# A graph layer on one core: the gathers' extra wait is taken out, and four list slots of two tiles of the seventh pair become one-hot products

## The chip, the cores and the metric

One Trainium2 chip, of which the kernel uses one core. The metric is device time in microseconds; a kernel's time is the median of its runs. The engines are TensorE (PE, with its weight loads PEld), VectorE (DVE), ScalarE (ACT), GpSimd (POOL) and SyncE (SP, which here only issues transfers).

## What is computed

16 graphs of 1024 nodes with 64 channels and a 0/1 adjacency (about 9 neighbours a node). Each node's own row is layer-normed and cut at zero; some edges are dropped by a rule on their rank; over a node's remaining neighbours (itself among them) three quantiles of each channel are taken and weighted; a small MLP follows.

```python
h = jnp.maximum(_layernorm(x, axis=-1), 0.0)
neigh = (adj_ > 0) & ~eye
rank = jnp.cumsum(ni, axis=-1) - ni
...
rem = neigh & (sk > 1) & (rank % sk == sk - 1) & mask[:, :, None]
rem = rem | jnp.swapaxes(rem, 1, 2)
adj_d = jnp.where(rem, 0.0, adj_)
...
s = jnp.sort(vals, axis=2)
for tau, w in zip((0.25, 0.5, 0.75), (0.25, 0.5, 0.25)):
    pos = tau * (nv - 1)
    ...
    agg = agg + w * (v_lo + frac * (v_hi - v_lo))
out = h + agg
y = jax.nn.relu(out @ W1 + b1) @ W2 + b2
return x + y * mask
```

## The kernel before

**Stages.** The graphs (batches 0 to 15) go in pairs (0 to 7). For each batch, `load` takes the adjacency in eight tiles of 128 rows, `drop` and `keep` find the edges that stay, `order` sorts the nodes by their number of neighbours, and `collect` writes for each node the list of its neighbours' numbers: `lists[b]`, the tile idx, which is done at L1186. The normed rows h go to a table in HBM, gtab.

**Gathers.** A pair's sorted nodes stand in eight tiles of 128 nodes, in four classes (`CLASSES`, L65): tile 0; tiles 1, 2, 3; tiles 4, 5; tiles 6, 7. For each class there is a buffer in SBUF, g0, g1, g4 and g6, with a slot for each place in the list; g0 and g1 exist twice, g4 and g6 once. One gather (L1329, an indirect transfer that POOL prepares) fills one slot of one tile of one graph: 128 rows of 64 values, by one column of the list. A pair needs 126 of them; the last pair 70.

**Picks.** For the last pair (pair 7) the first slots of tiles 0 to 5 (`LEAST`, L67: 8, 4, 4, 4, 4, 4) are not gathered. Every node there has that many neighbours, and the rows are taken from SBUF instead: `begin_pick` (L1344) loads the two graphs' table from HBM (xt), splits each value into three bf16 terms (terms) and turns the list into f32 (index). `pick` (L1370) works in rounds of eight slots. PE spreads eight list columns over the partitions (rowsT), ACT copies them (rows), DVE compares them with the node numbers in eight instructions of 128x1024 (hot, L1389), PE multiplies hot by the terms (got, L1398, 64 products a round), and ACT puts the bytes of got into the slots (L1409, L1410). There are seven rounds. hot has one buffer, shared with other tiles of the tag "wide"; index has the two buffers of the tag "keys".

**Sorts.** `sort` (L1414) runs a sorting network over a class's slots with DVE's min and max (L1437, L1442, L1434); the wanted places are weighted (L1457 on ACT, L1459 on DVE) and summed by PE (L1463). Behind many of DVE's instructions `opened` (L853) sets a memset of one column, called pause. 32 nodes of each graph with very many neighbours are sorted apart, eight graphs at a time, in gg. `one_hot`, `sums` and `mlp` bring the result back to node order and make the output.

**The order.** `weave` decides only which instruction is written down first. Then `arrange` (L713) takes all instructions as a graph of dependencies, buffers among them, with a cost for each (`Step.cost`), and makes each engine's order by walks forwards and backwards over it (`ROUNDS`, L74); the walk with the shortest total stands. The order of each engine is fixed from then on. Behind the walks, two waits are set on POOL: each gather waits for the count of those issued before it (`paced`), and, the leash (L785 to L794), for a DVE instruction: the latest among those with waiters on other engines that the plan ends more than 25000 ns (`LEASH`) ahead of the gather's planned start.

```python
    shown = [s for s in sequence["DVE"] if s.tells]
    for s in sequence["POOL"]:
        while len(shown) > 1 and starts[shown[1].place] + shown[1].busy < starts[s.place] - LEASH:
            shown.pop(0)
```

The main loop (L1830) weaves the results of pair m - 1 with the lists of pair m + 1; at m = 7 the picks stand in place of the lists.

Of the kernel before, what the change touches and what calls it, by code (L numbers as in the profile page):

```python
# [47 lines left out]
NT = N // P  # L48
# [16 lines left out]
CLASSES = (((0,), 13), ((1, 2, 3), 11), ((4, 5), 9), ((6, 7), 7))  # L65

LEAST = (8, 4, 4, 4, 4, 4, 0, 0)  # L67
# [3 lines left out]
GROUP = 8  # L71
SLICE = P // GROUP
SECOND = 14
ROUNDS, LEASH = 6, 25000  # L74


TURNED = (0, 1, 3, 2, 0, 1, 3, 2)
# [635 lines left out]
def arrange(tc, runs, loose, tails, paced):  # L713

    steps, found, number = [], {}, {}
    for ins in list(tc.nc.cur_bb.bb.instructions):
        if type(ins).__name__.startswith("BassTile"):
            continue
        if ins.name in tails:
            at = found[ins.name] = found[tails[ins.name]]  # L720
            at.tail.append(ins)
            number[ins.name] = len(number)
            at.busy += 12
            continue
        found[ins.name] = Step(ins, len(steps))
        steps.append(found[ins.name])

    written, read, users, order = {}, {}, {}, {}
    for s in steps:
        for u in s.reads + s.writes:  # L730
            name = u.tile.name
            for o, other in written.get(name, ()):
                if u.meets(other):
                    s.before.add(o.place)
            for o, other in read.get(name, ()) if u in s.writes or u.psum else ():
                if u.meets(other):
                    (s.before if u in s.writes or o.engine != s.engine else s.behind).add(o.place)
        for u in s.writes:
            for table in (written, read):
                table[u.tile.name] = [e for e in table.get(u.tile.name, ()) if not u.covers(e[1])]  # L740
            written[u.tile.name].append((s, u))
        for u in s.reads:
            read.setdefault(u.tile.name, []).append((s, u))
        for u in s.reads + s.writes:
            if getattr(u.tile, "tag", None):
                if u.tile.name not in users:
                    order.setdefault(u.tile.tag, []).append(u.tile)
                users.setdefault(u.tile.name, []).append(s)
    for tiles in order.values():
        for k, t in enumerate(tiles):  # L750
            bufs = t.tag_meta.bufs
            first = users[t.name][0]
            if k:
                first.behind.add(users[tiles[k - 1].name][0].place)
            if k >= bufs:
                first.before.update(o.place for o in users[tiles[k - bufs].name])
            for o in users[t.name][1:]:
                if o is not first:
                    o.behind.add(first.place)
    close = {found[n].place: (found[run[0]].place, found[run[-1]].place) for run in runs for n in run[:-1]}  # L760
    for s in steps:
        for first, last in {close[p] for p in s.before if p in close}:
            if not first <= s.place <= last:
                s.before.add(last)
    for s in steps:
        s.behind -= s.before
        s.before.discard(s.place)
        s.behind.discard(s.place)
        for p in (*s.before, *s.behind):
            steps[p].after.append(s)  # L770

    for s in steps:
        s.tells = any(o.engine != s.engine for o in s.after if s.place in o.before)
    ranks, best = [float(s.place) for s in steps], None
    for _ in range(ROUNDS):
        sequence, starts, total = forward(steps, ranks)
        if best is None or total < best[0]:
            best = total, sequence, starts
        ranks = backward(steps, starts)
    _, sequence, starts = best  # L780

    for k, s in enumerate(s for s in sequence["POOL"] if s.ins.name in paced[1]):
        if k > 1:
            paced[1][s.ins.name].wait_op(paced[0], k - 1, "sem-ge")
    shown = [s for s in sequence["DVE"] if s.tells]  # L785
    for s in sequence["POOL"]:
        while len(shown) > 1 and starts[shown[1].place] + shown[1].busy < starts[s.place] - LEASH:
            shown.pop(0)
        if s.ins.name in paced[1] and starts[shown[0].place] + shown[0].busy < starts[s.place] - LEASH:
            tc.add_manual_dep(  # L790
                s.ins, shown[0].ins.name,
                mybir.DependencyInfo(mybir.DependencyClass.Sync, mybir.DependencyReason.DATA),
                reason="leash of the gathers",
            )  # L794
    for steps in sequence.values():
        alike = iter(sorted((i for s in steps for i in s.tail), key=lambda i: number[i.name]))
        line = [i for s in steps for i in (s.ins, *(next(alike) for _ in s.tail))]
        at = {ins.name: k for k, ins in enumerate(line)}
        for ins in line:
            if ins.name in loose and at[loose[ins.name]] < at[ins.name] - 1:  # L800
                tc.declare_no_dep(ins, loose[ins.name], reason="read in order by one engine")
        for ins, then in zip(line, line[1:]):
            tc.add_manual_dep(
                then, ins.name, mybir.DependencyInfo(mybir.DependencyClass.NoSync, mybir.DependencyReason.DATA),
                reason="order of the engine",
            )
# [3 lines left out]
def list_layer(  # L810
# [494 lines left out]
            turn[0] += 1  # L1305
            many = None if many is None else many - 1

    def opening(some, m=B // 2 - 1):

        tiles, slots = some  # L1310
        if (m, tiles) not in gathered:
            gathered[m, tiles] = wk.tile(
                [P, PLANS[slots][0], len(tiles), 2, C], F32, name=f"g{tiles[0]}", bufs=2 - tiles[0] // 4
            )

    def fetch(m, classes=CLASSES, halves=(0, 1)):

        for tiles, slots in classes:
            lo, n = tiles[0], len(tiles)
            held, order = PLANS[slots][:2]  # L1320

            def begin(h, tiles=tiles, lo=lo, n=n, slots=slots, held=held):
                opening((tiles, slots), m)
                nc.scalar.copy(gathered[m, tiles][:, slots - 1, :, h], owns[m][:, lo:lo + n, h])

            issued, given_out = paced

            def gather(h, slot, k, at, tiles=tiles, lo=lo):
                ins = nc.gpsimd.indirect_dma_start(  # L1329
                    out=gathered[m, tiles][:, slot, k - lo, h], out_offset=None, in_=tables[2 * m + h][0],  # L1330
                    in_offset=bass.IndirectOffsetOnAxis(ap=lists[2 * m + h][:, at:at + 1], axis=0),
                    element_offset=tables[2 * m + h][1], engine_sem=issued,
                )
                given_out[ins.ins.name] = ins
                return ins

            for h in halves:
                queue.append(partial(begin, h))
                for k in tiles:
                    for s, slot in enumerate(order[:FULL[k] + ((k, FULL[k]) in HOSTS)]):  # L1340
                        if m < pairs - 1 or s >= LEAST[k]:
                            queue.append(partial(gather, h, slot, k, PASSED[k] + s))

    def begin_pick():  # L1344

        first = wk.tile([P, NT], F32, name="first", bufs=1)
        nc.vector.tensor_tensor(first, own2.rearrange("p (t k) -> p t k", k=2)[:, :, 0], own2.rearrange("p (t k) -> p t k", k=2)[:, :, 1], OP.add)
        nc.vector.tensor_scalar(first, first, float(FRONT), None, OP.add)
        terms, index = [], []
        for h in range(2):  # L1350
            b = 2 * (pairs - 1) + h
            xt = wk.tile([P, NT, C], F32, name="xt", bufs=1)
            tab, at = tables[b]
            nc.sync.dma_start(
# [10 lines left out]
            f = wk.tile([P, PASSED[-1]], F32, name="index", tag="keys", bufs=2)  # L1365
            nc.scalar.copy(f, lists[b])
            index.append(f)
        return first, terms, index

    def pick(first, terms, index, wanted):  # L1370

        m = pairs - 1
        for n in range(0, len(wanted), 8):
            some = wanted[n:n + 8]
            rows = wk.tile([P, len(some), P], F16, name="rows", tag="dist", bufs=2)
# [16 lines left out]
            for at in range(0, len(some), 2):  # L1392
# [8 lines left out]
                    )  # L1401
                    for q in range(2) for j in range(NT)
                ])
                opening((tiles, slots))
                step = to[1] - to[0]
                end = to[1] + (1 if step > 0 else -1)
                line = gathered[m, tiles][:, to[0]:end if end >= 0 else None:step, k - tiles[0], h]
# [379 lines left out]
    def drain(*gens):  # L1787
        for g in gens:
            for _ in g:
                pass  # L1790
# [39 lines left out]
    for m in range(pairs + 1):  # L1830
# [15 lines left out]
            nc.vector.tensor_scalar(flag, fp, 0.0, None, OP.is_gt)  # L1846
        side = chain(*(prepare(b) for b in (2 * m + 2, 2 * m + 3) if b < B))
        if m == pairs - 1:
            side = pick(*begin_pick(), [
                (h, k, s) for tiles, _ in CLASSES[:3] for h in range(2) for k in tiles for s in range(LEAST[k])  # L1850
            ])
            for _ in range(20):
                next(side)
# [190 lines left out]
```

## Time and profile before

| | us |
|---|---|
| median of 3 runs | 1918.85 |
| the runs | 1901.87, 1927.52, 1918.85 |
| the profiled execution: its time | 1901.87 |
| its span, first to last instruction | 1900.1 |
| granted TensorE clock, mean | 0.809 |
| gathers (L1329) | 952, mean 1.039 |
| one-hot compares (L1389) | 56, median 0.480 |
| products of the picks (L1398) | 448 |
| lists of batches 12 to 15 done at (L1186) | 1349.7, 1376.5, 1528.6, 1593.0 |
| sort of pair 6: g0, g1, g4, g6 (first to last step starts) | 1567 to 1648, 1647 to 1696, 1698 to 1723, 1723 to 1736 |
| gathers of pair 6: g0, g1, g4, g6 | 1484 to 1524, 1524 to 1624, 1624 to 1679, 1679 to 1705 |
| gathers of pair 7 and of gg | 1705 to 1852 |
| last sort step starts | 1879.1 |

How to read it: the profile is of one execution, and times in it count from its first instruction. A row of a group gives line, engine, operation, out <- in, count, busy time and mean in ns of one, then the idle time of the engine just before the group and what ended it. A row of the waits gives the total in us, how often, and the longest. "issue" and "remote" name no engine. A row of the timeline ends with the idle time before it and its releaser in brackets. The stretches give each engine's busy time and the number of its instructions.

### The profile page before, as it was taken

How to read it: one execution, taken by the hardware profiler on the slowest of the kernel's cores; microseconds unless marked ns; L12 is line 12 of the kernel's file. 1: busy time of each engine (PE TensorE's matmuls, PEld its weight loads, DVE VectorE, ACT ScalarE, POOL GpSimd, SP SyncE). 2: the span in 40 equal slices, each digit the busy share in tenths (PEclk: the TensorE clock that was granted, in tenths of full speed). 3: DMA queues.
4: the chain of work that ended last, by engine and by line, in shares of the span. 5: the costliest groups of instructions: out<-in, count | busy, mean ns of one | idle time of the engine just before them, and what ended most of it. 6: DMA issues, size and time to landing. Idle time of an engine off the chain costs nothing. (4 is left out here: it accounts for less than half of the span.)

```text
span 1900.1 us, 30251 instructions
## 1 busy us (share of the span) xinstructions
PE 1228.6 (65%) x8995; PEld 770.5 (41%) x9011; DVE 1226.8 (65%) x5869; ACT 1069.1 (56%) x2869; POOL 1027.3 (54%) x991
## 2 busy tenths in 40 slices
PE   6637566577867587667664687655873678733847
PEld 4424344254444344344432444433542345511434
DVE  5515277653676758774658658586757745596895
ACT  7646356466663578355662657353673675323765
POOL 0354564644564646554557455465565645577780
PEclk9769689597888798878877798767986789866868
DMA  5423232212331214121322123231230110112110
GB/s 185 137 76 92 61 92 67 83 50 68 84 102 43 86 39 137 42 73 45 102 79 50 54 47 104 54 94 32 54 71 18 31 21 20 19 23 49 27 31 15
DMA packets 128832, 121.67 MB, mean 64 GB/s; under 512 B 95730, under 2 KB 96274, under 8 KB 128658
## 3 DMA queue, kind: packets, MB, share of 16 engines
q1 hardware_dynamic: 97106, 87.29, 15.3%
q0 software_dynamic: 31552, 32.36, 8.7%
q8 instruction: 73, 1.20, 0.3%
q14 instruction: 101, 0.83, 0.1%
HBM read 108.79 MB, written 9.05 MB: 62 GB/s over the span
## 5 line engine op out<-in xcount | busy, mean ns | idle before, releaser
L1329 POOL DMA_INDIRECT g<-gtab,idx x952 | 989.4, 1039 | 816.3 <-issue 211.8
L1437 DVE TENSOR_TENSOR g<-g 128x384 f32<-128x384 f32 (+2 forms) x659 | 310.9, 492 | 25.1 <-issue 10.7
L1442 DVE TENSOR_TENSOR g<-g 128x384 f32<-128x384 f32 (+2 forms) x659 | 310.1, 491 | 10.1 <-DMA gg<-g 6.0
L1142 PE MATMUL codeP<-pack,perm 128*128 128x332 bf16 x1024 | 191.7, 332 | 59.2 <-DVE perm L1117 38.3
L1045 ACT ACTIVATE dist<-rk,bias 128x512 f16<-128x512 f32 x256 | 169.2, 701 | 84.5 <-remote 44.2
L1068 ACT ACTIVATE kept<-kp 128x512 fp8e4<-128x512 f32 x224 | 133.4, 600 | 132.9 <-remote 61.1
L978 ACT ACTIVATE ne<-tp 128x512 fp8e4<-128x512 f32 x248 | 143.4, 612 | 102.7 <-remote 67.4
L965 PE MATMUL tp<-kb,sg 128*128 128x128 bf16 x1024 | 119.9, 250 | 98.7 <-issue 37.5
L1463 PE MATMUL acc<-g,kf 128*128 128x128 f32 (+2 forms) x472 | 146.2, 446 | 55.7 <-ACT g L1457 35.5
L1035 PE MATMUL rk<-kb,cnt 128*128 128x512 bf16 x256 | 113.7, 444 | 93.6 <-ACT dist L1045 47.4
L1142 PEld LDWEIGHTS <-perm 128*128 128x128 bf16 x1024 | 100.1, 105 | 151.5 <-DVE perm L1117 49.4
L1040 PEld LDWEIGHTS <-ne 128*128 128x128 fp8e4 x1024 | 91.0, 110 | 154.7 <-issue 131.1
L1046 DVE TENSOR_SCALAR rem<-dist,half 128x1024 bf16<-128x1024 f16 x128 | 62.9, 493 | 129.4 <-ACT dist L1045 120.0
L965 PEld LDWEIGHTS <-sg 128*128 128x128 bf16 x1024 | 89.2, 113 | 140.8 <-issue 119.6
L1071 PE MATMUL code<-kw,kept 128*128 128x17 fp8e5 x1024 | 66.2, 175 | 122.4 <-ACT kept L1068 74.5
L958 ACT ACTIVATE sg<-at 128x1024 bf16<-128x1024 f32 x122 | 130.6, 1070 | 4.8 <-DMA at<-in_adj_dram 4.7
L1457 ACT ACTIVATE g<-g,coef 128x64 f32<-128x64 f32 x336 | 87.8, 339 | 79.0 <-DVE g L1437 44.1
L1058 PE MATMUL kp<-ne,kw 128*128 128x512 fp8e4 x256 | 112.7, 441 | 23.0 <-ACT cnt L1007 8.4
L1071 PEld LDWEIGHTS <-kept 128*128 128x128 fp8e4 x1024 | 54.1, 102 | 175.8 <-ACT kept L1068 98.6
L856 DVE MEMSET pause<- 128x1 bf16 x2043 | 120.5, 59 | 2.3 <-issue 2.3
L1463 PEld LDWEIGHTS acc<-g,kf 128*128 128x128 f32 x472 | 87.5, 224 | 84.0 <-ACT g L1457 43.1
L1040 PE MATMUL rk<-kw,ne 128*128 128x128 fp8e5 x1024 | 120.5, 245 | 0.0
(202 smaller groups left out, 2489.2 us busy)
## 6 DMA issues: line engine op xcount, KB each, us to landing
at<-in_adj_dram SPq DMA_DIRECT2D x122, 512.0 KB
g<-gtab,idx POOLq DMA_INDIRECT x952
xt<-in_x_dram SPq DMA_DIRECT2D x16, 256.0 KB
y<-in_x_dram SPq DMA_DIRECT2D x16, 256.0 KB
gtab<-xt SPq DMA_DIRECT2D x16, 256.0 KB
out_dram<-y SPq DMA_DIRECT2D x14, 256.0 KB
spare<-in_adj_dram SPq DMA_DIRECT2D x6, 512.0 KB
gg<-g SPq DMA_DIRECT2D x32, 48.0 KB
```

Source lines behind the costliest of these rows:

```text
L856: tails[nc.vector.memset(pause[:, at:at + 1], 0.0).ins.name] = ins.ins.name
L958: nc.scalar.activation(sg, at, AF.Sign)
L965: run.append(nc.tensor.matmul(tp[:, s], sg[:, m * P:(m + 1) * P], ident16, start=(s == 0), stop=(s == 3 and t // 4 != n), skip_group_check ...
L978: nc.scalar.activation(to, tp, AF.Relu, saturate=False)
L1040: run.append(nc.tensor.matmul(rk[:, s * P:(s + 1) * P], ne[:, 4 * n + s, ts], upper, start=False, stop=(s == 3), skip_group_check=True,))
L1045: nc.scalar.activation(dist[:, n * HALF:(n + 1) * HALF], rk, AF.Abs, bias=bias[:, t:t + 1])
L1068: nc.scalar.activation(kept[:, 4 * n:4 * n + 4], kp, AF.Relu, saturate=False)
L1142: run.append(nc.tensor.matmul(flat, perm[:, t, k * P:(k + 1) * P], pack[:, t], start=False, stop=(t == NT - 1), skip_group_check=True,))
L1329: ins = nc.gpsimd.indirect_dma_start(out=gathered[m, tiles][:, slot, k - lo, h], out_offset=None, in_=tables[2 * m + h][0], in_offset=bass ...
L1437: nc.vector.tensor_tensor(at(f + k * df, df, many), pa, pb, OP.min if what == "<" else OP.max)
L1442: nc.vector.tensor_tensor(pa if back else pb, pa, pb, OP.max if what == "<" else OP.min)
L1463: nc.tensor.matmul(acc, ident32, lines[:, s], start=False, stop=(s == now[-1] and not ends), skip_group_check=True)
```

## The change

Two things, in one diff. The leash is deleted, with `LEASH` and `tells`. And `begin_pick` and `pick` take the pair as an argument: `picked(m)` says which tiles of a pair are picked, all for the last pair as before, and now tiles 4 and 5 for the pair ahead of it (pair 6). There the first four slots (`LEAST` is 4) of two tiles of two graphs, 16 in all, are no longer gathered. Their picks, two rounds of eight, are written down at the start of m = 7, ahead of the last pair's. `arrange` then orders everything anew by the same walks.

```diff
-ROUNDS, LEASH = 6, 25000
+ROUNDS = 6
...
-    for s in steps:
-        s.tells = any(o.engine != s.engine for o in s.after if s.place in o.before)
...
-    _, sequence, starts = best
+    sequence = best[1]
...
-    shown = [s for s in sequence["DVE"] if s.tells]
-    for s in sequence["POOL"]:
-        while len(shown) > 1 and starts[shown[1].place] + shown[1].busy < starts[s.place] - LEASH:
-            shown.pop(0)
-        if s.ins.name in paced[1] and starts[shown[0].place] + shown[0].busy < starts[s.place] - LEASH:
-            tc.add_manual_dep(
-                s.ins, shown[0].ins.name,
-                mybir.DependencyInfo(mybir.DependencyClass.Sync, mybir.DependencyReason.DATA),
-                reason="leash of the gathers",
-            )
...
                     for s, slot in enumerate(order[:FULL[k] + ((k, FULL[k]) in HOSTS)]):
-                        if m < pairs - 1 or s >= LEAST[k]:
+                        if s >= LEAST[k] or k not in picked(m):
                             queue.append(partial(gather, h, slot, k, PASSED[k] + s))
...
+    def picked(m):
+
+        return range(NT) if m == pairs - 1 else CLASSES[2][0] if m == pairs - 2 else ()
...
-            b = 2 * (pairs - 1) + h
+            b = 2 * m + h
...
-    def pick(first, terms, index, wanted):
-
-        m = pairs - 1
+    def pick(m, first, terms, index, wanted):
+
...
         if m == pairs - 1:
-            side = pick(*begin_pick(), [
+            first = first_nodes()
+            drain(pick(pairs - 2, first, *begin_pick(pairs - 2), [
+                (h, k, s) for h in range(2) for k in picked(pairs - 2) for s in range(LEAST[k])
+            ]))
+            side = pick(pairs - 1, first, *begin_pick(pairs - 1), [
                 (h, k, s) for tiles, _ in CLASSES[:3] for h in range(2) for k in tiles for s in range(LEAST[k])
             ])
```

`first_nodes` holds the two instructions that begin_pick had at its start (the node numbers of each tile).

More of the change, by code (lines that the diff above doesn't have):

```diff
@@ L777, in arrange @@
         if best is None or total < best[0]:
-            best = total, sequence, starts
+            best = total, sequence
         ranks = backward(steps, starts)
-    _, sequence, starts = best
+    sequence = best[1]
     for k, s in enumerate(s for s in sequence["POOL"] if s.ins.name in paced[1]):
@@ L1306, in issue, with opening @@
             many = None if many is None else many - 1
-    def opening(some, m=B // 2 - 1):
+    def opening(some, m):
         tiles, slots = some
@@ L1340, in fetch, with first_nodes @@
                     for s, slot in enumerate(order[:FULL[k] + ((k, FULL[k]) in HOSTS)]):
-                        if m < pairs - 1 or s >= LEAST[k]:
+                        if s >= LEAST[k] or k not in picked(m):
                             queue.append(partial(gather, h, slot, k, PASSED[k] + s))
-    def begin_pick():
+    def picked(m):
+        return range(NT) if m == pairs - 1 else CLASSES[2][0] if m == pairs - 2 else ()
+    def first_nodes():
         first = wk.tile([P, NT], F32, name="first", bufs=1)
@@ L1348, in begin_pick @@
         nc.vector.tensor_scalar(first, first, float(FRONT), None, OP.add)
+        return first
+    def begin_pick(m):
         terms, index = [], []
         for h in range(2):
-            b = 2 * (pairs - 1) + h
+            b = 2 * m + h
             xt = wk.tile([P, NT, C], F32, name="xt", bufs=1)
@@ L1367, in begin_pick @@
             index.append(f)
-        return first, terms, index
-    def pick(first, terms, index, wanted):
-        m = pairs - 1
+        return terms, index
+    def pick(m, first, terms, index, wanted):
         for n in range(0, len(wanted), 8):
@@ L1403, in pick @@
                 ])
-                opening((tiles, slots))
+                opening((tiles, slots), m)
                 step = to[1] - to[0]
```

## The prediction

> **What bounds the kernel now.** I read the page first, then the waits of POOL, the timeline of POOL where they are, and last the stretches and DVE's waits of the end. All times are of the profiled execution: span 1900.1 us, its own time 1901.87 us.
>
> ```profile
> PE 1228.6 (65%) x8995; PEld 770.5 (41%) x9011; DVE 1226.8 (65%) x5869; ACT 1069.1 (56%) x2869; POOL 1027.3 (54%) x991
> ...
> L1329 POOL DMA_INDIRECT g<-gtab,idx x952 | 989.4, 1039 | 816.3 <-issue 211.8
> ```
>
> No engine is full over the span. The row of the gathers says more: 952 of them, 1.039 us each, and 816.3 us in which POOL stood idle ahead of them. The smallest gap in POOL's timeline is 0.30 us, also between instructions that carry no leash, so 952 x 0.30 = 286 us is floor and 530 us is waiting for something.
>
> ```profile
> POOL g L1329 <- DVE g L1442: 69.4, 47, 12.7
> ...
> POOL g L1329 <- DVE pause L856: 59.4, 63, 5.6
> POOL g L1329 <- DVE num L1084: 30.4, 5, 12.3
> ```
>
> In these waits of POOL a gather is released by a sort step of an older tile, by a one-column memset, by a count of neighbours. No gather reads any of these: that is the leash. It is what holds POOL back, and not data, as one gather of pair 5 shows in POOL's timeline, beside the list of batch 12 in DVE's:
>
> ```profile
> 1438.30 1.22 POOL L1329 DMA_INDIRECT g<-gtab,idx  x1 [10.48 <-DVE num L1084]
> ...
> 1483.99 0.94 POOL L1329 DMA_INDIRECT g<-gtab,idx  x1 [0.30 <-issue]
> ```
>
> ```profile
> 1349.42 0.25 DVE L1186 SCALAR_TENSOR_TENSOR idx<-bit,low 128x104 int32<-128x104 f32 x1
> ```
>
> The list of batch 12 is done at 1349.67, and its first gather goes at 1483.99, behind the gathers of pair 5. So POOL works some 134 us behind its lists, with a queue of work that is ready, and still waits. Who waits for the gathers? In the view of their line only POOL itself does (75.1 us, 201 times); DVE's sorts name no gather. The end, where the last lists have come (batch 15's at 1592.7), decides:
>
> ```profile
> 1606.00:1736.00 130.00, 59.39 (x430) 45.35 (x429) 94.14 (x437) 48.37 (x165) 85.15 (x80) 0.74 0.12 22
> 1736.00:1800.00 64.00, 47.98 (x222) 26.40 (x224) 45.28 (x181) 37.47 (x76) 45.47 (x37) 0.81 0.20 44
> 1800.00:1850.00 50.00, 23.46 (x121) 18.75 (x119) 48.17 (x113) 35.45 (x94) 41.31 (x28) 0.62 0.14 29
> 1850.00:1880.00 30.00, 24.05 (x102) 12.42 (x104) 23.75 (x80) 20.02 (x70) 3.73 (x4) 0.89 0.03 5
> ```
>
> The columns are PE, PEld, DVE, ACT, POOL. From 1800 to 1850 DVE is full (48.17 of 50) and its last sort step starts at 1879.1; POOL's last gather starts at 1851.1. Both run to the end side by side, DVE with more work behind it. DVE's idle time from 1606 to 1880 is 35.9 + 18.7 + 1.8 + 6.3 = 62.7 us, and its waits there are
>
> ```profile
> DVE hot L1389 <- PE got L1398: 13.0, 1, 13.0
> DVE at_p L1569 <- remote: 11.5, 1, 11.5
> DVE g L1437 <- issue: 8.6, 2, 7.6
> DVE few L1744 <- ACT o L1742: 5.2, 1, 5.2
> DVE g L1437 <- remote: 4.1, 3, 2.1
> DVE hot L1389 <- PE rowsT L1379: 3.9, 3, 2.9
> DVE hot L1389 <- ACT rows L1385: 3.1, 1, 3.1
> ```
>
> hand-overs of the picks and of the outputs, not gathers. So I read the end as DVE's own order, with POOL close behind.
>
> **The leash goes** (831 of 952 gathers wait for DVE in the built program before, 27 of 936 after). It frees up to 530 us of POOL's idle time, and POOL will run ahead until a list or a buffer stops it. Worked from the rows: pair 6's g4 buffer is free when pair 5's sort of it ends (1514) and its memset has run (1550), so its gathers could start near 1550 and started at 1624, 74 us later. Those ahead of them in POOL's order would be through: pair 6's 78 of g0 and g1 from its second list (1376.5) on, by 1.34 us, end at 1481. What is late next is nothing on DVE, whose order is fixed and which waited for no gather. So the price on the path is 0, and the cover is that DVE always came later than the gathers (g1 of pair 6 landed by 1626, sorted from 1647). Bounds: a loss I exclude for DVE's own steps, since the 128x384 step takes 0.55 us with a gather beside it or without; a gain is at most the 6.7 us of unnamed waits at the sorts and memsets from 1606 to 1880 (4.1 + 2.6).
>
> [...]
>
> **Sixteen gathers go**: tiles 4 and 5, four slots, two graphs. By the mean, 16 x (1.039 + 0.30) = 21.4 us of POOL; by the row of the end (1663 to 1853: 1.265 us each), 16 x (1.265 + 0.30) = 25.0 us. With POOL off the path they are worth 0, with POOL on it 25.0.
>
> **Two rounds of picks come.** PE: 32 transposing passes by 0.275 us (112 stand for the 56 slots of before) and 128 products by 0.14 us (32 took 4.56 us at 1657) = 8.8 + 17.9 = 26.7 us, against 70.6 us that PE is idle from 1606 to 1736. ACT: 4 copies of rows by 0.586, 8 pairs of copies of got by 0.303 + 0.378, two casts of terms by 0.613 + 1.050, two of index by 0.27 = 2.3 + 5.4 + 3.3 + 0.5 = 11.5 us, against 81.6 us idle there. DVE: 16 compares by 0.48 and 16 memsets by 0.06 = 8.6 us; DVE is the path, so they count whole. SP: two loads of 256 KB, 0.37 us each to issue; behind them stand pair 7's own two loads, the small copies into gapart and gg, and from 1739.7 on the outputs. In the new order one of pair 7's loads stands behind copies of g0 of pair 6, so pair 7's picks wait for them; before, SP issued nothing from 1601 to 1711, so that has room. A cost there, if the cover fails, is a round of picks (below).
>
> The index of batch 13 takes the buffer of batch 15's keys, so the second round can't start before 1593; in the new order it stands there, with DVE's next compares.
>
> **The order is made anew.** DVE's is almost unchanged up to its instruction 4,896 (near 1605). Then the sort of g4 of pair 6 begins at 4,928 and not 5,174, and that of g0 of pair 6 ends late, between others. Four independent sorts then lie between the compares of the picks, in the stretch 1606 to 1736 where DVE was idle for 35.9 us. Fills of none to all of it give 0 to -35.9 us. I take half, 18 us: the nearest row is the full stretch of 1800 to 1850, where such mixed sorts left 1.8 us of 50, but 13.0 and 7.6 us of the idle time are waits for PE, which order alone may not fill.
>
> Sum against the profiled 1901.87: + 8.6 - 18.0 = -9.4, so 1892.5 us. The profiled execution was the fastest of three; the median is 1918.85, 17.0 higher. The forecast of a median is 1918.85 - 9.4 = **1909 us**; its own range is none to all filled, +8.6 to -27.3: 1892 to 1927.
>
> **Rivals.** (1) POOL was the path at the end. For it: from 1663.5 to 1855 POOL goes without rest but for some 11 us above its floor (the longest wait is 5.12), and the chain of waits runs through the gathers of gg from 1717 to 1735. Against: DVE names no gather. Then 25.0 us go at the least, and with the lead on top as much as DVE's idle time less its new work, 62.7 - 8.6 = 54 us: 1865 to 1894. (2) Slower: the rounds of picks run in series on DVE, PE and ACT. Compares started at 1607.9, 1619.8, 1632.2 and 1642.1, so a round takes 11.4 us, of which 4.3 are DVE's. Two more are 22.8 us if no sort fills them: 1942. It decides once the filled idle time is under 8.6 us, and passes 2% only with another 16 us lost to the new order. (3) The change does next to nothing: leash never last, picks hidden: 1919, within 5.
>
> **How the numbers follow.** Forecast 0.50, POOL the path 0.20, rounds in series 0.20, nothing 0.10. The three runs of before lie 25.7 us apart, so 2% (38 us: under 1880 or over 1957) is about what can be told from no change. Faster by that: over half of case 1 and a little of the forecast, 0.13; slower: a third of case 2 and a trace of others, 0.08; within: 0.79. The range takes in most of case 1 and all of case 2: 1870 to 1942.
>
> **What would show it.** Right: POOL's waits on DVE nearly gone and its gathers of pair 6 done before 1650; DVE's idle time from batch 15's list to its last sort step under 55 us; compares x72 of 0.48 us. Wrong: DVE's sorts now wait for gathers or for got (case 2), or DVE's busy share stays and the end moves with POOL's last gather (case 1). Should the time before batch 15's list move by over 10 us, my reading that the leash costs nothing on the way there is wrong.

## The result, and the profile after

| | before | after |
|---|---|---|
| median, us | 1918.82 (4 runs, 1901.87 to 1927.52) | 2534.12 (4 runs, 2529.10 to 2538.11) |
| ratio | | 1.322, 95% interval 1.3126 to 1.3313 |
| span of the profiled execution | 1900.1 | 2527.4 |
| granted TensorE clock, mean | 0.809 | 0.724 |
| list of batch 15 done at | 1593.0 | 2173.4 |

The change made the kernel a third slower. From the page of the changed kernel: the engines' busy times; two rows of the span in 40 slices, DVE and POOL (a digit is the busy share of a slice in tenths); the chain of waits by engine; two groups (busy time, mean ns of one, then idle time ahead of the group).

```profile
PE 1224.9 (48%) x9155; PEld 766.4 (30%) x9171; DVE 1219.8 (48%) x5901; ACT 1067.5 (42%) x2895; POOL 943.8 (37%) x975
...
DVE  6223177024509361292465716329543192339597
...
POOL 0624433572360727406217171630544405430400
...
another core or an unknown queue 35%; ACT 20%; issue 17%; PE 17%; DVE 8%; DMA 1%; DVEq 0%; SPq 0%; ACTq 0%
...
L1317 POOL DMA_INDIRECT g<-gtab,idx x936 | 908.4, 971 | 1437.1 <-issue 756.2
L1432 DVE TENSOR_TENSOR g<-g 128x384 f32<-128x384 f32 (+2 forms) x659 | 310.4, 491 | 57.9 <-remote 56.7
```

No engine works longer than before: DVE 1219.8 us against 1226.8, PE 1224.9 against 1228.6, and a sort step takes 491 ns. So the added 627 us of span are idle time on every engine. Where POOL's digit is high, DVE's is mostly low, and the other way round. The stretches show it in us (stretch, its length, busy time of PE, PEld, DVE, ACT, POOL, each with its instructions but the length; then the clock and the DMA):

```profile
200.00:300.00 100.00, 23.42 (x193) 13.73 (x192) 15.62 (x62) 25.15 (x49) 59.53 (x63) 0.59 0.23 59
300.00:400.00 100.00, 71.54 (x666) 47.74 (x664) 74.70 (x350) 63.29 (x186) 19.94 (x20) 0.86 0.22 66
...
1600.00:1700.00 100.00, 21.38 (x182) 14.32 (x182) 14.64 (x86) 12.85 (x32) 54.63 (x58) 0.55 0.12 23
1700.00:1800.00 100.00, 67.70 (x514) 44.26 (x514) 96.06 (x480) 53.73 (x142) 13.19 (x12) 0.81 0.18 53
```

With some 60 gathers in 100 us, DVE does 15 us of work; with 12 to 20 of them, 75 to 96. The waits of the changed kernel say of what kind the idle time is (waiter, releaser, us in total, times, longest; the last two rows are the kernel before, in the same order of steps as the first and third):

```profile
DVE keys L1139 <- remote: 190.4, 10, 51.9
...
ACT kept L1056 <- remote: 178.1, 18, 26.5
...
ACT ne L966 <- remote: 153.1, 23, 18.2
...
DVE keys L1151 <- remote: 25.6, 8, 5.1
ACT ne L978 <- remote: 67.4, 21, 13.3
```

The first of these stood at 25.6 us before and stands at 190.4 now, and its longest wait went from 5.1 to 51.9. The profile names no engine that ended them. One such stretch in the timeline of all engines (it is put down to "issue", which names none either):

```profile
718.56 1.22 PE L1641 MATMUL yp<-b2r,ones_r 128*128 128x256 f32 x2 [21.07 <-ACT h L1627]
...
730.93 0.94 POOL L1317 DMA_INDIRECT g<-gtab,idx  x1 [0.30 <-issue]
731.82 0.60 ACT L966 ACTIVATE ne<-tp 128x512 fp8e4<-128x512 f32 x1 [13.31 <-issue]
...
732.47 0.59 PE L1023 MATMUL rk<-kb,cnt 128*128 128x512 bf16 x1 [12.69 <-issue]
```

ACT's step waits for PE alone. PE's last work ends at 719.8 and PE does nothing until 732.47, so what ACT waits for had happened 12.0 us or more before it started. POOL meanwhile issues a gather each 1.25 us without a rest. Once ACT has run, PE follows within 0.05 us of its end.

### The profile page after: what moved, and what is told of

It reads as the page before. It is cut to its first block, busy times and chain, and to the rows that moved or that the text cites. A ratio compares the mean times of both kernels' runs of the same rounds, so it can differ in the third digit from the quotient of the medians.

```text
span 2527.4 us, 30574 instructions
## 1 busy us (share of the span) xinstructions
PE 1224.9 (48%) x9155; PEld 766.4 (30%) x9171; DVE 1219.8 (48%) x5901; ACT 1067.5 (42%) x2895; POOL 943.8 (37%) x975
## 4 chain that ended last, share of the span: by engine, by line
another core or an unknown queue 35%; ACT 20%; issue 17%; PE 17%; DVE 8%; DMA 1%; DVEq 0%; SPq 0%; ACTq 0%
ACT dist L1033 4%; PE codeP L1130 4%; ACT sg L946 3%; ACT ne L966 2%; ACT kept L1056 2%; DVE g L1432 2%; DVE g L1437 2%; PE acc L1458 2%; ACT g L1452 1%; PE high L1580 1%; ACT waste L1228 1%; PE kp L1051 1%; PE tp L953 1%; PE kp L1047 1%
## 5 line engine op out<-in xcount | busy, mean ns | idle before, releaser
L1317 POOL DMA_INDIRECT g<-gtab,idx x936 | 908.4, 971 | 1437.1 <-issue 756.2
L1130 PE MATMUL codeP<-pack,perm 128*128 128x332 bf16 x1024 | 200.4, 341 | 73.3 <-DVE perm L1105 28.3
L953 PE MATMUL tp<-kb,sg 128*128 128x128 bf16 x1024 | 112.6, 240 | 188.5 <-ACT dist L1033 80.7
L1139 DVE MAX8 keys<-codeP 128x8 f32<-128x128 f32 x128 | 36.8, 292 | 252.5 <-remote 190.4
```

Source lines behind the costliest of these rows:

```text
L953: run.append(nc.tensor.matmul(tp[:, s], sg[:, m * P:(m + 1) * P], ident16, start=(s == 0), stop=(s == 3 and t // 4 != n), skip_group_check ...
L1130: run.append(nc.tensor.matmul(flat, perm[:, t, k * P:(k + 1) * P], pack[:, t], start=False, stop=(t == NT - 1), skip_group_check=True,))
L1317: ins = nc.gpsimd.indirect_dma_start(out=gathered[m, tiles][:, slot, k - lo, h], out_offset=None, in_=tables[2 * m + h][0], in_offset=bass ...
```

## The experiments

The theory (1): unbroken gathers on POOL make the other engines' signals to each other come late, and the leash broke the runs of gathers up. The rivals: (2) the new order and the picks of pair 6; (3) not that POOL stops, but that each gather carries a second wait.

**The two parts apart.** The first kernel is before without the block of the leash, the second is after with that block put back (25000 ns), the third is before with

```diff
-ROUNDS, LEASH = 6, 25000
+ROUNDS, LEASH = 6, 250000
```

> The kernel before without the leash, nothing else: no picks in pair 6, the same order on every engine. Theory 1 (the leash breaks up POOL's bursts of gathers, and an unbroken burst makes PE, DVE and ACT receive each other's signals late): 2450 to 2600 us, as after (2534), with DVE's busy time still within 1% of 1226.8 us and the waits that name no engine several times those of before. Theory 2 (the new order and the pick rounds of pair 6 do it): 1900 to 1940 us. Theory 3 (each gather loses an instruction for its second wait, and that alone spaces them): as theory 1 here.

> The changed kernel with the leash of before put back (25000 ns): the picks of pair 6 and the new order alone. Theory 1: 1880 to 1940 us, where my forecast of the picks stood (1909 us, and 1942 us for rounds in series). Theory 2: 2450 to 2600 us. Theory 3: as theory 1 here.

> The kernel before with LEASH at 250000 ns in place of 25000: the later gathers still wait for a DVE instruction, but for one that the plan ends a quarter of a millisecond ahead, so the wait should be met long before POOL comes to it. POOL ran 134 us behind its lists before. Theory 1 (what counts is that POOL stops): 2450 to 2600 us. Theory 3 (what counts is that there is a second wait on the instruction): 1900 to 1960 us. Theory 2 (the new order): 1900 to 1940 us.

Measured, with before at 1905.97: without the leash 2566.68, ratio 1.348 (1.3399 to 1.3561); picks with the leash 1905.59, ratio 0.998 (0.9948 to 1.0014); the long leash 2552.46. The page of the kernel without the leash:

```profile
PE 1223.0 (48%) x8995; PEld 766.9 (30%) x9011; DVE 1214.8 (48%) x5869; ACT 1058.0 (41%) x2869; POOL 965.5 (38%) x991
...
L1319 POOL DMA_INDIRECT g<-gtab,idx x952 | 920.9, 967 | 1490.2 <-issue 715.4
```

The same picture as after, with no pick of pair 6 in it. So the leash's loss is the whole of it, and rival 2 falls. That the leash broke up the runs of gathers can be counted in the traces: of the 986 gathers of before, 240 stand in runs of 16 or more with under 0.6 us between one gather's end and the next one's start, and the longest such run has 46; without the leash 806 stand in such runs, and the longest has 66. The third run tells rival 3 nothing: with 250000 ns only 29 gathers of the built program still wait for DVE, so it removed the waits a second time.

**A rest without DVE.** Three memsets of one private column behind each gather, or 24 behind each eighth; a wait for the transfer two before; and no gathers at all. All four are built on before without its leash; the kernel with 24 memsets has `range(24 if len(given_out) % 8 == 0 else 0)` in the first of these lines; in the last one POOL fills the slots with list numbers, so the quantiles are taken over these.

```diff
+                for _ in range(3 if len(given_out) % 1 == 0 else 0):
+                    tails[nc.gpsimd.memset(breath[:, len(tails) % 16:len(tails) % 16 + 1], 0.0).ins.name] = ins.ins.name
```
```diff
             tc.add_manual_dep(
-                s.ins, shown[0].ins.name,
+                s.ins, given[k - 2].ins.name,
...
```
```diff
-                ins = nc.gpsimd.indirect_dma_start(
...
+                ins = nc.gpsimd.tensor_copy(gathered[m, tiles][:, slot, k - lo, h], lists[2 * m + h][:, at:at + 1].to_broadcast([P, C]))
+                for _ in range(8):
```

> Without the leash, but POOL sets three memsets of one private column behind every list gather; the order of the instructions is otherwise that of the kernel without the leash, and no gather waits for DVE. A memset of one column took 0.10 to 0.12 us on POOL, so a gather should come each 1.6 to 1.8 us in place of 1.25 (952 of them: 1520 to 1710 us, which still fits). Theory 1 says that it is the unbroken run of gathers that does the harm and not the missing knowledge of DVE's progress: if a short rest between any two is enough, 1900 to 2000 us; if a rest must be long enough for the other engines' signals to get through (the leash's rests lasted several us), 2300 to 2570 us. A theory that POOL must be kept from running ahead (gathers early against DVE's work) expects 2450 to 2570 us here.

> The same memsets, but 24 behind every eighth list gather in place of three behind each: POOL gathers for about 10 us without a rest and then rests 3 to 4 us; the mean rate is that of the three memsets behind each. If the mean rate of gathers decides, the time is that of the kernel with three memsets behind each, within 2%. If the stall only begins after some gathers in a row and a long rest clears it, this one is the faster of the two (1900 to 2000 us); if a signal can get through in any short gap, it is the slower, with the bursts' 10 us lost each time.

> Without the leash, but each list gather waits until the transfer of the gather two before has landed (before it was eight, by the queue's lanes). If it is the number of gathers under way that holds up the other engines' signals, 1900 to 2000 us. If POOL's preparing of gathers back to back does it whatever is under way, 2450 to 2570 us, with gathers still 1.25 us apart; should a landing take over 2.5 us, the gathers come farther apart and this run measures a spacing too.

> Without the leash, and each of the 952 list gathers is replaced by a copy of its list column into the slot and eight memsets of one private column, all on POOL: POOL is as busy, back to back, with the same waits for lists and buffers, but no indirect transfer is made (the quantiles are then taken over list numbers, not over the neighbours' rows). If a busy POOL is what holds up the others, 2300 to 2570 us. If it is the preparing or the transfer of gathers (theory 1), 1850 to 1930 us, with waits that name no engine below those of before.

Measured: 1470.85, 1560.54, 1887.84 and 1460.70 us. But the kernel before took 1452.52 us beside them, and not 1906. None of the four profiles has a wait on "remote" among its groups of waits. So these runs met other surroundings; I call them the 1450 surroundings, after the time of before, and those of the first runs the 1900 ones. By the one run of before beside them, one run each, the ratios are 1.013, 1.074, 1.300 and 1.006. The third run is no case of late signals. Its POOL waits for landings, as its row says:

```profile
L1325 POOL DMA_INDIRECT g<-gtab,idx x952 | 986.6, 1036 | 820.4 <-DMA g<-gtab,idx 706.8
```

**Is the leash worth anything in the 1450 surroundings?**

> The kernel without the leash once more, together with the one with three memsets behind each gather, because the kernel before took 1452.5 us beside the last four runs and 1906 us beside the first three. Where the kernel before takes about 1900 us: 2500 to 2600 us, as the first time. Where it takes about 1450 us, no wait of the last four profiles named no engine for long, so the others' signals were not held up there: then theory 1 expects that the leash has nothing to do and that its loss costs nothing, 1420 to 1480 us; if unbroken gathers hold up signals there too, over 1600 us.

> The kernel without the leash and with three memsets behind each gather once more. Where the kernel before takes about 1900 us, this is the question that the last runs left open: 1450 to 1900 us if a rest of about half a microsecond between any two gathers lets the signals through, 1900 to 2400 us if it helps in part, 2400 to 2600 us if only rests of several microseconds do. Where the kernel before takes about 1450 us: 1471 us within 1%, as before.

Before took 1444.53 us; without the leash 1444.98, ratio 0.9995 (0.998 to 1.0009); with the memsets 1467.72, ratio 1.016 (1.0106 to 1.022). The page of the kernel without the leash, in these surroundings:

```profile
PE 1103.7 (76%) x9011; PEld 708.1 (49%) x9011; DVE 1220.8 (85%) x5869; ACT 1041.9 (72%) x2869; POOL 1050.6 (73%) x991
...
DVE  5647699978899899978699898998699779979775
...
POOL 0277777777777777777777777777777777778881
...
L1319 POOL DMA_INDIRECT g<-gtab,idx x952 | 1009.6, 1060 | 353.3 <-DMA g<-gtab,idx 282.4
```

It is the same program as in the first experiment, on 1443.5 us in place of 2556.8. POOL gathers almost without a rest over the whole span (985 of its 986 gathers stand in runs of 16 or more, the longest of 219), and DVE is busy beside it all the time. An unbroken run of gathers is therefore not enough for the harm; the surroundings have to be the 1900 ones as well.

**The change again, and the memsets.**

> The changed kernel itself once more, beside the kernel before. Where before takes about 1900 us: 2534 us within 1.5%. Where it takes about 1445 us, the leash was worth nothing (0.9995), and what is left is the picks of pair 6: they were worth 0.998 with the leash in the slower surroundings, so I expect 0.98 to 1.01, 1416 to 1460 us; POOL has 16 gathers less and DVE and PE two rounds more, as in my forecast.

> The kernel without the leash and with three memsets behind each gather, for the case that before takes about 1900 us here, which the last two tries did not meet. In the two profiles where gathers held the others up, only 2 to 3 of the 16 landing signals of a gather show up in the trace while gathers follow each other at 1.25 us, against 12 to 15 in the others. If it is the rate of these signals that the core cannot take, a gather each 1.6 us (10 a us in place of 13) gives 1500 to 2100 us; if any unbroken run of gathers does it, 2400 to 2600 us. Where before takes about 1445 us: 1468 us within 1%.

Here before took 1871.45; after 2511.30, ratio 1.342 (1.336 to 1.3489); with the memsets 2410.48, ratio 1.288 (1.2796 to 1.2962). But the memsets were no rest. The timeline of POOL in that run:

```profile
417.71 0.17 POOL L1327 MEMSET breath<- 128x1 bf16 x3
418.03 0.94 POOL L1320 DMA_INDIRECT g<-gtab,idx  x1
418.98 0.17 POOL L1327 MEMSET breath<- 128x1 bf16 x3
419.30 0.94 POOL L1320 DMA_INDIRECT g<-gtab,idx  x1
```

They went into the 0.30 us that a gather stands behind the one before anyway: the gathers came each 1.27 us, where I had expected 1.6 to 1.8. So the effect of a fixed rest has not been tried. Why the ratio is 1.288 and not 1.342 as for after beside it isn't shown. The 12 to 15 steps that the expectation gives for the other profiles are miscounted: the table at the end has 15.8 in the 1450 surroundings and 5.6 for before in the 1900 ones. The 16 of the expectation is the most that one gather has on record in the trace of before, where 130 of 986 have that many.

**Other leashes, and no gathers.** Before with LEASH at 6000 and at 80000, and the kernel without gathers again.

> The kernel in which each list gather is replaced by a copy of the list column and eight memsets on POOL, once more (the quantiles are taken over list numbers, not over the neighbours' rows). Where the kernel before takes about 1900 us: if the gathers are what holds the others up, about 1460 us as in the other surroundings, and the whole difference between the surroundings is theirs; if something else is slower there, 1700 to 1950 us. Where before takes about 1450 us: 1460 us again.

> The kernel before with LEASH at 6000 ns in place of 25000 (860 of 978 gathers wait for DVE in place of 831). Where before takes about 1900 us: if what helps is that POOL is held close to DVE's progress, 1700 to 1890 us; if only the presence of a second wait helps, within 1% of before. Where before takes about 1450 us: a shorter leash can only hold POOL up, 1445 to 1550 us.

> The kernel before with LEASH at 80000 ns: 677 gathers wait for DVE, more than two in three, but POOL may be 80 us of the plan ahead. (At 250000 ns only 29 waits were left, about as many as without the leash, so that run was the leash's removal over again.) Where before takes about 1900 us: if POOL must be held close, 2200 to 2500 us; if the second wait on each gather is what helps, 1900 to 2050 us. Where before takes about 1450 us: within 1% of before.

Before took 1445.46 us. Without gathers 1461.15; the short leash 1455.73, ratio 1.007 (1.0037 to 1.0108); the long one 1442.50. Where the leash has nothing to do, a short one costs a little. These three runs met the 1450 surroundings, in which they leave their question open.

> The kernel without list gathers (their slots are filled with list numbers by POOL, which is kept as busy by memsets), a third time. Where the kernel before takes about 1900 us: about 1460 us if the gathers hold the others up, 1700 to 1950 us if not. Where before takes about 1450 us: 1460 us.

> The changed kernel once more. Where the kernel before takes about 1450 us, my forecast of the two parts (the leash nothing, the picks and the new order -9.4 us in sum) would give a ratio of 0.985 to 1.005, and no run there has shown otherwise. Where before takes about 1900 us: 1.32 to 1.35, as in the first runs.

Before took 1440.68; without gathers 1462.06; **after 1436.42, ratio 0.9958 (0.9943 to 0.9972)**. Where the gathers hold nobody up, the change is worth 6 us by the ratio and 4 by the medians, near my forecast of its parts. Another execution of after, one of ten, took 3228.63 us at a granted clock of 1.0; the ratio leaves it out, and nothing on record says what happened in it. From the page of after there:

```profile
PE 1119.6 (78%) x9171; PEld 718.6 (50%) x9171; DVE 1227.0 (85%) x5901; ACT 1052.5 (73%) x2895; POOL 1039.4 (72%) x975
...
L1317 POOL DMA_INDIRECT g<-gtab,idx x936 | 1001.1, 1070 | 350.8 <-DMA g<-gtab,idx 278.6
```

> The kernel without list gathers (their slots are filled with list numbers by POOL, which is kept as busy by memsets). Where the kernel before takes about 1900 us: about 1460 us if the gathers hold the others up, 1700 to 1950 us if something else does. Where before takes about 1450 us: 1460 us.

Before took 1866.72, and the kernel without gathers 1478.56 us, 1.2% over its 1461 in the 1450 surroundings. Its page:

```profile
PE 1114.0 (75%) x9011; PEld 711.9 (48%) x9011; DVE 1267.2 (86%) x5869; ACT 1046.5 (71%) x2869; POOL 531.3 (36%) x8607
...
DVE  5756899987999979998699897999889775998995
...
L1320 POOL CAST g<-idx 128x64 f32<-128x64 int32 x952 | 345.4, 363 | 815.7 <-PE acc L1451 339.1
```

This run, a single one, shows where the time goes. Take the list gathers away, and what separates the two surroundings is gone but for 17 us. Of the 1867 us of before, some 388 were therefore lost to gathers already, with the leash in place. One thing was not as announced: POOL was busy for 531 us, not as long as with gathers, so that a busy POOL alone does it is made unlikely and not excluded. Nor does the run tell what about a gather costs the others time: its preparing, its transfer, the signals of its landing or their recording all went with it.

> The kernel before with LEASH at 80000 ns: 677 of 978 gathers still wait for DVE. Where the kernel before takes about 1900 us: 2200 to 2500 us if POOL must be kept close to DVE's progress, 1870 to 2050 us if a second wait on the gather is what helps. Where before takes about 1450 us: within 1% of before, as the last time.

Before took 1446.87; this 1447.47, ratio 0.9985 (0.9962 to 1.0009). It met the surroundings in which it can tell nothing. No kernel was shown to beat before in both surroundings: the picks with the leash are at 0.998 in the 1900 ones, where the interval (0.9948 to 1.0014) takes in no difference at all, and the change as it is at 0.9958 in the 1450 ones.

## Why the prediction was wrong

**The step that failed** is the price of the leash: "So the price on the path is 0", with the reason "a loss I exclude for DVE's own steps, since the 128x384 step takes 0.55 us with a gather beside it or without". The reason is true: the 128x384 step takes 0.55 us before and without the leash, and its group, smaller steps among them, stands at 490 to 494 ns in every run with list gathers. But it bounds the length of steps, and not the time between them. What the runs showed in its place is 1.348 (1906 to 2567 us) for this one edit, all of it in idle time of the engines. That the loss could come from a resource that is no engine's work should have stood as a rival with its own price; none of my three had it.

**The rows that said so were there**, in the profile of before. I listed "DVE at_p L1569 <- remote: 11.5" and put it to the hand-overs of the picks. Its place in the timeline of before:

```profile
1757.18 0.94 POOL L1329 DMA_INDIRECT g<-gtab,idx  x1 [0.31 <-issue]
1758.43 0.94 POOL L1329 DMA_INDIRECT g<-gtab,idx  x1 [0.30 <-issue]
1762.23 0.59 ACT L1621 COPY highs<-high 128x512 f32<-128x512 f32 x1 [10.86 <-remote]
1762.33 0.62 DVE L1569 TENSOR_SCALAR at_p<-iota,node 128x512 bf16<-128x512 f16 x2 [11.52 <-remote]
...
1764.50 0.94 POOL L1329 DMA_INDIRECT g<-gtab,idx  x1 [5.12 <-DVE at_p L1569]
```

ACT and DVE stand for 11 us while POOL issues six more gathers 1.25 us apart, and go on 3 us after the last of them, POOL being stopped by the leash. Here the leash held POOL when the others had come to a stand. "ACT ne <- remote: 67.4" and its like, 21 groups in before's waits and 361.8 us over all engines, gave the size of the matter.

**A second step that failed.** "It frees up to 530 us of POOL's idle time" took POOL's waits for DVE to be the leash's doing. Without the leash, in the same surroundings, POOL's idle time ahead of the gathers did not fall from 816.3 us but rose to 1490.2. In the 1450 surroundings it is 353.3 us without the leash, and hardly more with one that is even shorter (6000 ns):

```profile
L1329 POOL DMA_INDIRECT g<-gtab,idx x952 | 1006.8, 1058 | 366.9 <-DMA g<-gtab,idx 132.0
```

So a leash by itself costs POOL about 14 us there. In the 1900 surroundings the DVE that POOL waited for was itself late, as in the stretch above; how much of the 530 us that is has not been measured.

**What held.** The floor of 286 us that I had named makes up most of the 353.3. The leash is worth nothing to the path in the 1450 surroundings: 0.9995. The 16 gathers, the two rounds and the new order, -9.4 us in sum, came out at 0.998 with the leash (-3.6 us of 1906, between -9.9 and +2.7) and, with the leash gone where it is worth nothing, at 0.9958 (-6.1 us of 1441). The terms were less exact: DVE's added work is 1227.0 - 1220.8 = 6.2 us against 8.6, and its idle time between batch 15's list and the last sort step fell by 8.0 us (41.3 to 33.3), where I had taken 18 (both from the profiles of the kernel without the leash and of after, in the 1450 surroundings). They make -1.8 us; in these two profiles batch 15's list also came 2.9 us earlier, where I had expected no gain. That the sum came out near is in part luck.

**The test I had set** gave the right answer: batch 15's list was to move by under 10 us, and moved by 580. The sentence for that case was "my reading that the leash costs nothing on the way there is wrong". The rivals (POOL the path, rounds in series, nothing) were not what happened.

**Gathers and the length of steps.** The group of sort steps stands at 490 to 494 ns with gathers dense or thin, and it is the gather that grows: 967 ns where DVE is busy for 48% of the span and 1060 ns where it is for 85%, in one and the same program, though in different surroundings. These are lengths of instructions; they say nothing on the time between them, where the loss was.

**What stays open.** Which property of the surroundings makes the difference: times of before of 1867 to 1919 us and of 1441 to 1453 us came in turns, and chips numbered 0 and 11 stand in the records of both. By which way a gather delays the signals: below is what the traces show, and it is no proof. A rival that no run tested is the recording itself: every time on record has a span and a granted clock beside it, as the profiler gives them, so no run shows what these kernels take when nothing is recorded. And why the leash helped: that it ties POOL to DVE's progress fits the rows above, but the two leash lengths that were to tell this from a second wait met the 1450 surroundings, and a fixed rest was not achieved.

## What to carry to other kernels

That no step is longer and that nobody waits for a transfer does not make an engine's burst free: look for stretches in which all other engines stand still at once beside it, with waits that name no engine, and price the edit by what such a stretch costs each time. A wait that looks useless may be what keeps a burst short; take it out alone, in a run of its own, before anything is built on its absence. Run the kernel before beside each experiment: here it moved between 1441 and 1919 us from one set of runs to the next, and an edit that cost 35% in one set changed nothing in another.

## What the runs showed of the hardware

The landing of a gather shows in the traces as separate steps of its lane's semaphore. I counted those on record for the eight lanes and divided by the gathers of all kinds (986, after 970, and 34 in the kernel without list gathers):

| kernel | before's time beside it | span | landing steps on record for each gather |
|---|---|---|---|
| without the leash | 1444.5 | 1443.5 | 15542 / 986 = 15.8 |
| after | 1440.7 | 1439.1 | 15338 / 970 = 15.8 |
| before | 1918.8 | 1900.1 | 5538 / 986 = 5.6 |
| without the leash | 1906.0 | 2556.8 | 2243 / 986 = 2.3 |
| after | 1918.8 | 2527.4 | 2375 / 970 = 2.4 |
| no list gathers | 1866.7 | 1476.3 | 131 / 34 = 3.9 |

In the trace of before no gather has more than 16 steps on record until the next one of its lane, and 130 of the 986 have 16. In the 1450 surroundings the mean is 15.8; in the 1900 ones the kernels with list gathers have 2.3 to 5.6, and the longer the span, the fewer. The kernel without the leash is one program, with the same waits for landings, at 15.8 and at 2.3, and it ran to its end both times. I take it that the steps came there too and that most of them are missing from the record; no trace shows it. The kernel without list gathers has 3.9 steps for each of its 34 other gathers, and this run alone of the four of that kernel has waits on "remote" (29.2 us in 7 waits, the longest 7.3). So few steps on record and waits on "remote" went together in the runs of this table. How far the two are one thing, since the profile infers releasers from the semaphore events on record, was not shown, and that the waits are long isn't explained by it. That both come from one path that is overfull, up to 16 steps each 1.25 us, is a guess that no run here tested.
